# Five blocks of x loaded by four transfers of unequal row counts

## The chip, the cores and the metric

The kernel runs on one core of one Trainium2 chip. The metric is the device time in microseconds; the median of three runs of the kernel before is 1354.09 us (1353.96 to 1354.46). A core has the compute engines PE (matmul), DVE (VectorE), ACT (ScalarE) and GpSimd (POOL), the queue engine SP (SyncE), and 16 DMA engines, which move all data between HBM and the on-chip memory. Transfers are issued on queues: SP's queue appears in the profile as q1, ACT's as q10.

## The reference

For a batch of 4096 rows with 32 fields of 64 numbers, each pair of fields (i, j), i < j, has its own 64 x 64 matrix. Field i is multiplied by the matrix of the pair and the result, elementwise, by field j.

```python
def _L0_rec_ref(inputs, W):          # inputs (4096, 32, 64), W (496, 64, 64), float32
    F = inputs.shape[1]
    idx_i, idx_j = np.triu_indices(F, k=1)      # 496 pairs
    vi = inputs[:, idx_i, :]
    vj = inputs[:, idx_j, :]
    vidots = jnp.einsum('bpd,pde->bpe', vi, W)
    return vidots * vj                # (4096, 496, 64)
```

The input is 33.55 MB of x and 8.13 MB of W; the output is 520.09 MB.

## The kernel before

The batch is cut into 16 blocks of 256 rows. A block stands in the on-chip memory as 128 partitions, each with two batch rows (`NB = 2`); one partition of a block is a contiguous run of 16,384 bytes in HBM. There are two buffers for x. Block 0 and block 1 are loaded by SP's queue at the start, the others, 2 to 15, in the loop by ACT's queue, each in a single transfer of 128 rows.

```python
    xpool = ctx.enter_context(tc.tile_pool(name="xpool", bufs=2))
    tpool = ctx.enter_context(tc.tile_pool(name="tpool", bufs=4))
    opool = ctx.enter_context(tc.tile_pool(name="opool", bufs=3))
    # [cut]
    def new_x(blk: int):
        xs[blk] = xpool.tile([P, 1 + NB * F, D], F32, tag="xs", name=f"xs_{blk}")
        nc.gpsimd.memset(xs[blk][:, 0, :], 0.0)

    def load_x(blk: int, eng, k0: int = 0, k1: int = NB):
        src = rows_of(x, blk).rearrange("(p k) f d -> p (k f) d", k=NB)
        eng.dma_start(out=xs[blk][:, 1 + k0 * F : 1 + k1 * F, :], in_=src[:, k0 * F : k1 * F, :])
    # [cut]
    loads = {place[blk * NB, LATE]: blk + 1 for blk in range(2, NBLK - 1)}   # blocks 3 to 15
    loads[place[LEAD, LATE]] = 2
    # [cut: blocks 0 and 1 and the weights are loaded by SP's queue]
```

A block has two tiles of 128 batch rows (`t`). For each tile the fields are transposed on PE, and for each run of pairs PE multiplies by the weights; DVE, or ACT and GpSimd together, multiply the result by field j and write it to a buffer `ot`. There are three such buffers. A tile's output is cut into five groups of pairs; a group is stored by one transfer on SP's queue, of 128 rows with 23,040, 24,832, 25,344, 26,880 and 26,880 bytes. So a block has ten stores and one load.

```python
    for s, (t, st) in enumerate(sched):
        # [cut]
        if s in loads:
            new_x(loads[s])
            load_x(loads[s], nc.scalar)
        # [cut: transpositions and weights that are due]
        if pa == base:
            ots[t] = opool.tile([P, cap, D], F32, tag="ot", name=f"ot_{t}_{g}")
        # [cut: matmuls into ps]
        if i in aside and c0 == 0 and s not in no_aside:
            tmp = tpool.tile([P, CH, 2, E2], F32, tag="tmp", name=f"tmp_{s}")
            nc.scalar.copy(tmp, src)
            nc.gpsimd.tensor_mul(dst, tmp, xj)
        else:
            nc.vector.tensor_mul(dst, src, xj)
        # [cut]
        if pa + m in ends:
            nc.sync.dma_start(out=..., in_=ot[:, n0 - base : pa + m - base, :])
```

Of the kernel before, what the change touches and what calls it, by code (L numbers as in the profile page):

```python
# [12 lines left out]
def kernel(  # L13
# [16 lines left out]
    nc = tc.nc  # L30

    B, F, D = x.shape
    P = 128
    NB = 2
# [16 lines left out]
    cuts = [*range(0, NP, P), NP]  # L51
# [12 lines left out]
    xs = {}  # L64

    def rows_of(dram: bass.AP, blk: int) -> bass.AP:
        return dram[blk * NB * P : (blk + 1) * NB * P]

    def new_x(blk: int):

        xs[blk] = xpool.tile([P, 1 + NB * F, D], F32, tag="xs", name=f"xs_{blk}")
        nc.gpsimd.memset(xs[blk][:, 0, :], 0.0)  # L72

    def load_x(blk: int, eng, k0: int = 0, k1: int = NB):
        src = rows_of(x, blk).rearrange("(p k) f d -> p (k f) d", k=NB)
        eng.dma_start(out=xs[blk][:, 1 + k0 * F : 1 + k1 * F, :], in_=src[:, k0 * F : k1 * F, :])  # L76


    wflat = w.rearrange("p d e -> p (d e)")
# [4 lines left out]
    def load_w(c: int, eng=nc.sync):  # L84

        a, b = wrows[c]
        pool, tag = ((opool, "ot"), (opool, "ot"), (const, "w3"), (const, "w3"))[c]
        raw[c] = pool.tile([P, D * D], F32, tag=tag, name=f"raw_{c}")
        eng.dma_start(out=raw[c][: b - a, :], in_=wflat[a:b])

    def order_w(c: int, k: int, copy):
        r = wrows[c][1] - wrows[c][0]
        rp = tpool.tile([P, EU, 2, D], F32, tag="tmp", name=f"rp_{c}_{k}")
        src = raw[c][:r, :].rearrange("p (d h e) -> p e h d", h=2, d=D)
        copy(rp[:r], src[:, k * EU : (k + 1) * EU])  # L95
        return rp

    def turn_w(c: int, k: int, rp, copy):
        r = wrows[c][1] - wrows[c][0]
        if c not in wT:  # L100
            wT[c] = const.tile([P, r, E2], F32, tag=f"w{c}", name=f"wT_{c}")
        pt = psum.tile([P, EU, P], F32, tag="ps", name=f"ptw_{c}_{k}")
        for n in range(EU):
            nc.tensor.transpose(  # L104
                pt[:, n, :r], rp[:r, n].rearrange("p h d -> p (h d)"), ident[:r, :r]
            )
        copy(wT[c][:, :, k * EU : (k + 1) * EU], pt[:, :, :r].rearrange("p e r -> p r e"))  # L107

    def turn_x(blk: int, k: int, q: int, copy):

        pt = psum.tile([P, RUN, P], F32, tag="ps", name=f"ptx_{blk}_{k}_{q}")
        for n in range(RUN):
            s = k * F + q * RUN + n
            nc.tensor.transpose(  # L114
                pt[:, n, :], xs[blk][:, s : s + 2, :].rearrange("p f d -> p (f d)"), ident
            )
        xT = xtpool.tile([P, RUN, P], F32, tag="xT", name=f"xT_{blk}_{k}_{q}")
        copy(xT, pt)  # L118
        return xT
# [41 lines left out]
    loads = {place[blk * NB, LATE]: blk + 1 for blk in range(2, NBLK - 1)}  # L161
    loads[place[LEAD, LATE]] = 2

    new_x(0)
    load_x(0, nc.sync, 0, 1)
    load_w(0)
    load_w(1)
    load_x(0, nc.sync, 1, NB)
    load_w(2)
    new_x(1)  # L170
    load_x(1, nc.sync)

    v, p, a = nc.vector.tensor_copy, nc.gpsimd.tensor_copy, nc.scalar.copy
# [9 lines left out]
    for s, (t, st) in enumerate(sched):  # L183
        blk, kt = divmod(t, NB)
        g, i, c0, m = steps[st]
        if s in loads:
            new_x(loads[s])
            load_x(loads[s], nc.scalar)
        for what, *args in due.get(s, ()):
            if what == "x":  # L190
                xT[tuple(args)] = turn_x(*args, a)
            elif what == "turn":
                turn_w(*args, rps.pop(tuple(args)), a)
            else:
                c, k = args
                rps[c, k] = order_w(c, k, (v, v, p, v)[c] if k % 2 == 0 else (v, v, p, a)[c])
                if (c, k) == (2, NU - 1):
                    load_w(3, nc.scalar)

        base, end = groups[g]  # L200
        pa = p0[i] + c0
        if pa == base:
            ots[t] = opool.tile([P, cap, D], F32, tag="ot", name=f"ot_{t}_{g}")
        ot = ots[t]
        ps = psum.tile([P, 2, CH, E2], F32, tag="ps", name=f"ps_{s}")
        for c, (lo, hi) in enumerate(wrows):
            lo, hi = max(pa, lo), min(pa + m, hi)
            if lo < hi:
                for h in range(2):
                    n = i + 1 - h  # L210
                    nc.tensor.matmul(  # L211
                        ps[:, h, lo - pa : hi - pa, :],
                        xT[blk, kt, n // RUN][h * D : (h + 1) * D, n % RUN, :],
                        wT[c][h * D : (h + 1) * D, lo - wrows[c][0] : hi - wrows[c][0], :],
                        start=True,
                        stop=True,
                    )
        o = pa - base
        j = 1 + kt * F + i + 1 + c0
        dst = ot[:, o : o + m, :].rearrange("p m (h e) -> p m h e", h=2)  # L220
        src = ps[:, :, :m, :].rearrange("p h m e -> p m h e")
        xj = xs[blk][:, j : j + m, :].rearrange("p m (h e) -> p m h e", h=2)
# [7 lines that stand above are left out]
        ends = (p0[2], end) if s < NS and (t, g) == (0, 0) else (end,)  # L230
        if pa + m in ends:
            n0 = p0[2] if len(ends) > 1 and pa + m == end else base
            nc.sync.dma_start(  # L233
                out=rows_of(out, blk).rearrange("(p k) n d -> p k n d", k=NB)[:, kt, n0 : pa + m, :],
                in_=ot[:, n0 - base : pa + m - base, :],
            )
# [27 lines left out]
```

## Time and profile before

| what | value |
|---|---|
| time, median of 3 | 1354.09 us |
| span of the profiled execution | 1353.3 us |
| mean granted TensorE clock | 0.948 |
| moved from and to HBM | 562.92 MB in DMA packets, mean 416 GB/s |
| x loads by ACT's queue | 14 of 2048 KB, 16.6 us each from issue to landing (median) |
| stores by SP's queue | 161, 16.4 us from issue to landing (median) |
| issue of an x load on ACT | 351 ns (median) |

How to read it: the profile counts, for each engine, the time in which it had an instruction at work. "Share of 16 engines" in the DMA rows is the time that packets took, divided by 16 times the span. A row of the waits names the engine and line that stood idle, what released it, the total time, the number of times and the longest. The trace also has a record for each DMA packet (queue, start, duration, bytes). A row of a transfer is one packet; each DMA engine that took part in a transfer leaves one more record, of 4 bytes, when its share is done. The records do not name the DMA engine.

### The profile page before, as it was taken

How to read it: one execution, taken by the hardware profiler on the slowest of the kernel's cores; microseconds unless marked ns; L12 is line 12 of the kernel's file. 1: busy time of each engine (PE TensorE's matmuls, PEld its weight loads, DVE VectorE, ACT ScalarE, POOL GpSimd, SP SyncE). 2: the span in 40 equal slices, each digit the busy share in tenths (PEclk: the TensorE clock that was granted, in tenths of full speed). 3: DMA queues.
4: the chain of work that ended last, by engine and by line, in shares of the span. 5: the costliest groups of instructions: out<-in, count | busy, mean ns of one | idle time of the engine just before them, and what ended most of it. 6: DMA issues, size and time to landing. Idle time of an engine off the chain costs nothing.

```text
span 1353.3 us, 17856 instructions
## 1 busy us (share of the span) xinstructions
PE 1180.3 (87%) x7424; PEld 690.9 (51%) x7424; DVE 956.9 (71%) x1262; ACT 374.1 (28%) x367; POOL 530.2 (39%) x246
## 2 busy tenths in 40 slices
PE   6989889889799897988879989888987989988994
PEld 4556545545455454555445545454554545545552
DVE  5778768767677676776757777676775767767774
ACT  3432222222232232222222222222222222223221
POOL 1813424444243443433444334433434434344431
PEclk9989999989999898999989999899998999989997
DMA  9999999999999999999999999999999999999997
GB/s 386 370 426 408 424 427 431 428 432 431 418 414 419 433 412 418 422 413 426 428 407 422 417 425 410 423 421 407 425 410 426 419 422 427 401 432 428 415 417 319
DMA packets 26273, 562.92 MB, mean 416 GB/s; under 512 B 2912, under 2 KB 2912, under 8 KB 3040
## 3 DMA queue, kind: packets, MB, share of 16 engines
q1 hardware_dynamic: 24048, 530.59, 92.4%
q10 hardware_dynamic: 2144, 31.20, 5.5%
q8 instruction: 58, 0.95, 0.3%
q14 instruction: 23, 0.19, 0.0%
HBM read 41.68 MB, written 520.09 MB: 415 GB/s over the span
## 4 chain that ended last, share of the span: by engine, by line
DMA 50%; PE 25%; DVE 17%; POOL 3%; issue 2%; ACT 0%; DVEq 0%; SPq 0%; POOLq 0%; ACTq 0%
DMA out_dram<-ot 50%; PE ps L211 20%; DVE ot L228 17%; PE ptx L114 4%; POOL ot L226 3%; PE ptw L104 1%; DMA raw<-in_L_rec_W_dram 1%; ACT tmp L225 0%; DVE rp L95 0%; POOL rp L95 0%; DVEq L228 0%; ACT wT L107 0%; SPq L76 0%; POOLq L226 0%; SPq L233 0%
## 5 line engine op out<-in xcount | busy, mean ns | idle before, releaser
L228 DVE TENSOR_TENSOR ot<-ps,xs 128x1024 f32<-128x1024 f32 (+15 forms) x1252 | 945.6, 808 | 364.7 <-DMA out_dram<-ot 185.9
L211 PE MATMUL ps<-wT,xT 64*128 64x512 f32 (+13 forms) x6272 | 1034.9, 473 | 132.8 <-DVE ot L228 121.3
L211 PEld LDWEIGHTS ps<-wT,xT 64*128 64x128 f32 x6272 | 563.7, 197 | 569.9 <-DVE ot L228 306.8
L226 POOL TENSOR_TENSOR ot<-tmp,xs 128x1024 f32<-128x1024 f32 x220 | 519.6, 2362 | 647.4 <-ACT tmp L225 457.1
L225 ACT COPY tmp<-ps 128x1024 f32<-128x1024 f32 x220 | 222.7, 1012 | 500.1 <-PE ps L211 459.6
L118 ACT COPY xT<-ptx 128x1024 f32<-128x1024 f32 x128 | 129.6, 1012 | 428.2 <-PE ptx L114 428.2
L114 PE MATMUL ptx<-ident,xs 128*128 128x128 f32 x1024 | 141.2, 281 | 18.5 <-DVE ot L228 9.9
L114 PEld LDWEIGHTS ptx<-ident,xs 128*128 128x128 f32 x1024 | 111.0, 142 | 64.3 <-issue 44.1
L72 POOL MEMSET xs<- 128x64 f32 x16 | 2.4, 152 | 148.6 <-DVE ot L228 148.6
L104 PE MATMUL ptw<-ident,rp 128*128 128x128 f32 (+1 forms) x128 | 19.2, 305 | 3.9 <-DVE rp L95 3.9
L104 PEld LDWEIGHTS ptw<-ident,rp 128*128 128x128 f32 (+1 forms) x128 | 16.2, 160 | 10.3 <-DVE rp L95 5.0
L107 ACT COPY wT<-ptw 128x1024 f32<-128x1024 f32 (+1 forms) x15 | 14.8, 984 | 21.4 <-PE ptw L104 21.4
L95 DVE COPY rp<-raw 128x1024 f32<-128x1024 f32 (+1 forms) x9 | 10.7, 1219 | 11.1 <-DMA raw<-in_L_rec_W_dram 11.1
L95 POOL COPY rp<-raw 128x1024 f32<-128x1024 f32 x4 | 8.0, 1994 | 0.1
L95 ACT COPY rp<-raw 112x1024 f32<-112x1024 f32 (+1 forms) x3 | 5.9, 1959 | 5.1 <-POOL ot L226 3.3
L107 DVE COPY wT<-ptw 128x1024 f32<-128x1024 f32 x1 | 1.2, 1224 | 3.3 <-PE ptw L104 3.3
L118 ACT ACT_TABLE_LOAD x1 | 1.3, 1283 | 0.7 <-PEq L251 0.7
masks.py:197 POOL MEMSET ident<- 128x128 f32 x1 | 0.2, 206 | 0.3 <-POOLq L251 0.3
masks.py:199 POOL TENSOR_SCALAR_AFFINE_SELECT ident<-ident 128x128 f32<-128x128 f32 x1 | 0.3, 295 | 0.0
L251 POOL MEMSET const-float32-0.0<- 128x1 f32 x1 | 0.1, 99 | 0.2 <-issue 0.2
L251 POOL MEMSET const-bfloat16-1.0<- 128x1 bf16 x1 | 0.1, 102 | 0.0
L251 POOL MEMSET const-uint8-127<- 128x1 uint8 x1 | 0.1, 102 | 0.0
(1 smaller groups left out, 0.1 us busy)
## 6 DMA issues: line engine op xcount, KB each, us to landing
out_dram<-ot SPq DMA_DIRECT2D x64, 3360.0 KB, 16.2
out_dram<-ot SPq DMA_DIRECT2D x32, 3168.0 KB, 15.4
out_dram<-ot SPq DMA_DIRECT2D x32, 3104.0 KB, 17.0
out_dram<-ot SPq DMA_DIRECT2D x31, 2880.0 KB, 16.4
xs<-in_r_inputs_dram ACTq DMA_DIRECT2D x14, 2048.0 KB, 16.6
raw<-in_L_rec_W_dram SPq DMA_DIRECT2D x3, 2048.0 KB, 14.3
xs<-in_r_inputs_dram SPq DMA_DIRECT2D x2, 1024.0 KB, 10.9
xs<-in_r_inputs_dram SPq DMA_DIRECT2D x1, 2048.0 KB, 24.6
```

The source lines that it names most:

```text
L72: nc.gpsimd.memset(xs[blk][:, 0, :], 0.0)
L95: copy(rp[:r], src[:, k * EU : (k + 1) * EU])
L104: nc.tensor.transpose(pt[:, n, :r], rp[:r, n].rearrange("p h d -> p (h d)"), ident[:r, :r])
L107: copy(wT[c][:, :, k * EU : (k + 1) * EU], pt[:, :, :r].rearrange("p e r -> p r e"))
L114: nc.tensor.transpose(pt[:, n, :], xs[blk][:, s : s + 2, :].rearrange("p f d -> p (f d)"), ident)
L118: copy(xT, pt)
L211: nc.tensor.matmul(ps[:, h, lo - pa : hi - pa, :], xT[blk, kt, n // RUN][h * D : (h + 1) * D, n % RUN, :], wT[c][h * D : (h + 1) * D, lo - ...
L225: nc.scalar.copy(tmp, src)
L226: nc.gpsimd.tensor_mul(dst, tmp, xj)
L228: nc.vector.tensor_mul(dst, src, xj)
L251: nc = _bacc.Bacc("TRN2", target_bir_lowering=False, num_devices=1)
```

## The change

The x load takes a list of row cuts. For block numbers that leave remainder 1 when divided by 3, the load in the loop is made by four transfers of 96, 25, 5 and 2 rows instead of one of 128; all four are issued on ACT's queue, one after the other. Its words say what it is for: "five of sixteen x blocks loaded by four transfers of ACT's queue with 96, 25, 5 and 2 rows, so that the first five DMA engines load more rows". What is computed stays the same, and so do all stores.

```diff
-    def load_x(blk: int, eng, k0: int = 0, k1: int = NB):
+    def load_x(blk: int, eng, k0: int = 0, k1: int = NB, cuts=(0, P)):
         src = rows_of(x, blk).rearrange("(p k) f d -> p (k f) d", k=NB)
-        eng.dma_start(out=xs[blk][:, 1 + k0 * F : 1 + k1 * F, :], in_=src[:, k0 * F : k1 * F, :])
+        for a, b in zip(cuts[:-1], cuts[1:]):
+            eng.dma_start(
+                out=xs[blk][a:b, 1 + k0 * F : 1 + k1 * F, :], in_=src[a:b, k0 * F : k1 * F, :]
+            )
+
+
+
+    UNEVEN = (0, 96, 121, 126, P)
 
@@
             new_x(loads[s])
-            load_x(loads[s], nc.scalar)
+            load_x(loads[s], nc.scalar, cuts=UNEVEN if loads[s] % 3 == 1 else (0, P))
```

## The prediction

> **What bounds the kernel now.** I read the page from the top: busy shares, then the DMA rows, the DMA queues, the chain that ended last, then the waits and, last, the single DMA records of the trace.
>
> ```profile
> span 1353.3 us, 17856 instructions
> PE 1180.3 (87%) x7424; PEld 690.9 (51%) x7424; DVE 956.9 (71%) x1262; ACT 374.1 (28%) x367; POOL 530.2 (39%) x246
> DMA  9999999999999999999999999999999999999997
> ...
> q1 hardware_dynamic: 24048, 530.59, 92.4%
> q10 hardware_dynamic: 2144, 31.20, 5.5%
> q8 instruction: 58, 0.95, 0.3%
> ...
> DMA 50%; PE 25%; DVE 17%; POOL 3%; issue 2%; ACT 0%; DVEq 0%; SPq 0%; POOLq 0%; ACTq 0%
> ```
>
> No compute engine is at its limit: the busiest, PE, has 87%. The 16 DMA engines have at least nine tenths in every slice but the last, and SP's queue (q1, the stores) and ACT's queue (q10, the x loads and one weight load) fill 97.9% of their time. So the bytes bound the kernel. The waits say through which buffers:
>
> ```profile
> DVE ot L228 <- DMA out_dram<-ot: 185.9, 84, 5.8
> ...
> POOL ot L226 <- DMA out_dram<-ot: 153.1, 59, 5.5
> ```
>
> DVE and GpSimd wait for a store to land, because the result goes through three buffers and a buffer is free only when its store has landed on all its DMA engines. The steady stage, over four blocks of x (compare columns five to eight, DMA share and GB/s):
>
> ```profile
> core 0: us, PE busy (x) PEld busy (x) DVE busy (x) ACT busy (x) POOL busy (x), PEclk, DMA share, GB/s
> 286.00:369.00 83.00, 72.51 (x456) 42.12 (x456) 58.91 (x78) 22.27 (x22) 33.07 (x15) 0.96 1.00 427
> 369.00:451.60 82.60, 74.07 (x456) 43.76 (x456) 58.68 (x78) 22.27 (x22) 33.18 (x15) 0.92 0.99 419
> 451.60:533.70 82.10, 72.75 (x456) 42.03 (x456) 59.02 (x78) 22.27 (x22) 33.21 (x15) 0.95 0.98 416
> 533.70:617.00 83.30, 72.34 (x456) 42.16 (x456) 58.64 (x78) 22.27 (x22) 33.23 (x15) 0.95 1.00 423
> ```
>
> One block takes about 82.7 us, of which PE is busy 73 us. The rest is a wait for stores.
>
> The page gives no time for each DMA engine, so I took the records apart. Each store leaves 16 small records of 4 bytes, one when each engine ends its share. From store 46 on (about 369 us) the median distance from the first of the 16 to the eighth is 0.1 us, to the fifteenth 1.7 us, to the sixteenth 6.3 us (5.2 to 9.5). So a single engine is far behind all others, always. Following the records that join end to end before such a last ending gives its rows:
>
> ```
> row of 26,880 bytes: 1,020 to 1,067 ns   (most other engines: 996)
> row of 23,040 bytes:   855 to   893 ns   (most other engines: 855)
> row of 16,384 bytes:   611 to   636 ns   (most other engines: 611)
> ```
>
> It is never idle in this stage: its next row starts 6 ns after the end of a store. The others are: they end a store 6 us earlier and wait until the slow one has set a buffer free. A block on an undisturbed engine is two times eight rows of 855, 921, 940, 996 and 996 ns and eight rows of 611 ns, less 3.5 ns for each row (they overlap by so much): 80.0 us. The measured 82.7 us is what the slow engine needs, 30 ns more for each of its 88 rows. So the time is the slow engine's sum of rows, and the other fifteen have up to 2.7 us of slack in a block.
>
> **What the Trainium skill says.** "DMA: Bandwidth & Descriptors", section "Why a DMA increments its semaphore by 16 and not by 1": a transfer from ACT's queue runs on the largest k up to 16 that divides its rows, and on the lowest-numbered k engines. No transfer of the kernel before shows a k below 16. Same page, "Queues, rings and completion order": an engine takes turns between its queues. The trace agrees: while an x load runs, rows of 996 ns and of 611 ns alternate on an engine. Same page, "Latency and other measured facts": engines 7 and 15 are usually slower than the rest in traces. The trace shows one slow engine; its records carry no number.
>
> **The change part by part.** By that rule 96 rows give 6 to each of 16 engines, 25 rows give 5 to each of engines 0 to 4, 5 rows one more to each of these, 2 rows one more to engines 0 and 1:
>
> ```
> engine      0, 1    2, 3, 4    5 to 15
> before       8         8          8
> after       13        12          6
> ```
>
> Bytes and the computation stay the same. The condition is a block number with remainder 1 by 3, and the load in the loop is called for blocks 2 to 15: that is 4, 7, 10 and 13. Block 1, the fifth of the title, is loaded ahead of the loop by SP's queue in one transfer. So four blocks change, not five. The built program agrees: ACT has 12 instructions more, three for each of four blocks.
>
> 1. Removed on engines 5 to 15: 4 blocks x 2 rows x 0.62 us (the slow engine's 611 to 636 ns) = 5.0 us each.
> 2. Added on engines 0 and 1: 4 x 5 x 0.611 = 12.2 us; on 2 to 4: 4 x 4 x 0.611 = 9.8 us. If none is the slow one this lies in their slack: 12 stages of about 82.7 us with up to 2.7 us each, some 32 us.
> 3. ACT: 12 more issues of about 351 ns (the median of its x loads) = 4.2 us in all; ACT is busy 28%, so nothing on the path.
> 4. New waits: the built program gives each small transfer a DMA semaphore, and makes it wait for that semaphore's earlier user, a store some eight transfers back. With three buffers that store has landed by then. The first transposition of such a block waits for four transfers in place of one, which land within about 25 us, when the block is needed only some 70 us after. Nothing.
> 5. A passing collision: after an uneven load engines 0 and 1 are 5 x 0.61 = 3.05 us later than before, the slow one 1.24 us earlier. It was 5.6 us behind the mass in the first store after a load, so it is 4.4 us behind, while 0 and 1 are at 3 to 4 us. Mostly the slow one still ends last. If an instruction fetch falls on 0 or 1 just then (a fetch held up its engine by about 1.8 us in the records at 432 us), it may cost a few tenths. I take 0.4 us in all.
>
> Sum, with the slow engine among 5 to 15: 1354.1 - 5.0 + 0.4 = 1349.5 us, 0.34% less.
>
> **The rivals.** (a) The slow engine is one of 0 to 4. Then its sum grows by 9.8 or 12.2 us, all on the path: 1364 to 1366 us. For it: when the stores start from rest, all 16 engines start within about 151 ns, in two groups, 7 within 32 ns and 9 from 53 ns on; in the steady stage the first group shows at most six, so the slow engine starts among the first seven. If they start in the order of their numbers, it is one of 0 to 6. Against it: the skill's page points at 7 and 15, the order may have nothing to do with numbers, and the split at exactly five engines makes sense only to someone who had seen the slow one above. I give it 17%. (b) The others are the bound anyway, through the collisions of step 5 or because engines 0 and 1 stay late: then the gain shrinks to 0 to 3 us, 1351 to 1354. Against it: 2.7 us of slack a block, and two even blocks after each uneven one. (c) PE or DVE take over as soon as stores are quicker: PE needs 73 of 82.7 us, and the gain is 1.2 us in each of four blocks; no room for this rival.
>
> **Range and chances.** The main case gives 1349 to 1350, a full gain without collisions 1349, a slow engine that gains more than its rows because its lag is shorter perhaps 1348; rival (b) up to 1354; rival (a), beyond, is the tail. I predict 1349.5 us, with 1347.5 to 1358 as the range for 8 in 10. A change of over 2% is 27 us either way, twice what the largest term can do: faster by over 2% 0.005, within 2% 0.985, slower 0.01.
>
> **What would show it.** In the changed kernel: ACT's x loads as ten of 128 rows and four each of 96, 25, 5 and 2; in the records of an uneven load, five engines with 12 or 13 rows of 16,384 bytes and eleven with 6; the sixteenth ending of a store still single and late, and the blocks with an uneven load about 1.2 us shorter, the others unchanged. If those blocks are 2.4 to 3.1 us longer, the slow engine is one of the first five. If they are no shorter and two engines end last together, it was the collision. A small transfer that lands 16 engines' worth of rows on more than five would make the row counts, and with them all terms, wrong.

## The result and the profile after

The changed kernel takes 1366.88 us (median of 4 runs, 1366.47 to 1367.77); the kernel before, run beside it, takes 1354.28 us (1353.96 to 1354.55). The ratio is 1.0094, with a 95% interval of 1.0077 to 1.0112. That is 12.6 us longer, where 4.6 us shorter was predicted: within 2%, but outside the range.

The page of the changed kernel, with the rows that were shown of the kernel before: span, busy shares, DMA slices, the queues (packets, MB, share of 16 engines) and the chain that ended last.

```profile
span 1364.9 us, 17876 instructions
PE 1185.5 (87%) x7424; PEld 692.4 (51%) x7424; DVE 957.4 (70%) x1262; ACT 374.0 (27%) x367; POOL 529.6 (39%) x246
...
DMA  9999999999999999999999999999999999999997
...
q1 hardware_dynamic: 24048, 530.59, 91.7%
q10 hardware_dynamic: 2192, 31.20, 5.5%
q8 instruction: 58, 0.95, 0.3%
...
DMA 49%; PE 27%; DVE 17%; POOL 4%; issue 2%; ACT 0%; DVEq 0%; SPq 0%; POOLq 0%; ACTq 0%
```

Nothing here looks like a new bound. Busy times of the compute engines and bytes are as before. Only q10 has 48 packets more: each engine that takes part in a transfer leaves an end record, and four loads in four parts leave 4 x (16 + 5 + 5 + 2) = 112 of them in place of 4 x 16 = 64. So 25 rows ran on five engines, 5 rows on five and 2 rows on two, as the rule that the prediction cited from the Trainium skill says ("DMA: Bandwidth & Descriptors", "Why a DMA increments its semaphore by 16 and not by 1"). The records count the engines but do not number them; the numbers below are those of the rule, by which a transfer takes the lowest. The waits are the old ones too (engine and line, what released it: us in all, times, longest; the change moves the lines by seven):

```profile
DVE ot L235 <- DMA out_dram<-ot: 177.4, 75, 5.8
POOL ot L233 <- DMA out_dram<-ot: 154.7, 59, 5.5
```

The loads are where the difference is. First the issues by size (issues, KB of each), then all issues of that line (times, then shortest, median and longest in ns, and first and last start in us):

```profile
xs<-in_r_inputs_dram ACTq DMA_DIRECT2D x10, 2048.0 KB
...
xs<-in_r_inputs_dram ACTq DMA_DIRECT2D x4, 1536.0 KB
...
xs<-in_r_inputs_dram ACTq DMA_DIRECT2D x4, 400.0 KB
...
xs<-in_r_inputs_dram ACTq DMA_DIRECT2D x4, 80.0 KB
xs<-in_r_inputs_dram ACTq DMA_DIRECT2D x4, 32.0 KB
```

```profile
L77 ACTq DMA_DIRECT2D xs<-in_r_inputs_dram x26: 285/364/1697, 135.7 to 1187.8; - x26
```

Four loads are split, not five, and the 26 issues are 12 more than before, at a median of 364 ns. Now four stages of one block each, the first and the fourth with a split load (columns as in the prediction):

```profile
core 0: us, PE busy (x) PEld busy (x) DVE busy (x) ACT busy (x) POOL busy (x), PEclk, DMA share, GB/s
274.40:360.10 85.70, 76.82 (x464) 44.31 (x464) 59.04 (x78) 23.04 (x23) 33.15 (x15) 0.90 0.98 415
360.10:442.90 82.80, 72.83 (x456) 41.95 (x456) 58.76 (x78) 22.34 (x23) 33.15 (x15) 0.96 0.99 419
442.90:525.50 82.60, 71.69 (x448) 40.85 (x448) 58.84 (x78) 21.43 (x22) 33.18 (x15) 0.96 0.99 418
525.50:610.80 85.30, 73.28 (x464) 43.08 (x464) 58.86 (x78) 22.97 (x23) 33.19 (x15) 0.96 0.97 408
```

The split blocks take 85.7 and 85.3 us, the others 82.8 and 82.6, and the DMA share of the split ones falls to 0.98 and 0.97, GB/s to 415 and 408: fifteen engines wait longer for one. The last endings of every tenth store, from the records, show it over the whole span:

```
us from one block's last ending to the next
before  83.29 82.68 82.07 83.25 82.67 82.69 83.23 82.67 82.69 82.65 82.68 80.25 77.67
after   85.73 82.71 82.64 85.35 82.68 82.65 85.68 82.68 83.05 86.55 82.04 80.85 77.66
        split             split             split             split
```

The four split blocks are longer by 2.44, 2.10, 2.45 and 3.90 us, 10.9 in all. The prediction had named the sign: longer by 2.4 to 3.1 us if the slow engine is one of the first five. Two of the four lie in that range, one below and one above. The slow engine's own records, end to end in the split block from 525.5 us on, say which rows it had. Before and between them lie rows of stores, not listed.

```
row of the 96-row transfer      613, 611, ... six in all, end record at 528.730
rows of the 25-row transfer     611, 618, 611, 611, 611,  end record at 537.828
row of the 5-row transfer       685,                      end record at 539.517
the 2-row transfer              no row and no end record
```

Six, five and one are 12 rows, and no share in the last transfer. By the rule this is engine 2, 3 or 4: the slow engine is among those that were given more rows.

### The profile page after: what moved, and what is told of

Read it like the earlier page. It is cut to its first block, busy times and chain, and to the rows that moved or that the text cites. A ratio compares the mean times of both kernels' runs of the same rounds, so it can differ in the third digit from the quotient of the medians.

```text
span 1364.9 us, 17876 instructions
## 1 busy us (share of the span) xinstructions
PE 1185.5 (87%) x7424; PEld 692.4 (51%) x7424; DVE 957.4 (70%) x1262; ACT 374.0 (27%) x367; POOL 529.6 (39%) x246
## 4 chain that ended last, share of the span: by engine, by line
DMA 49%; PE 27%; DVE 17%; POOL 4%; issue 2%; ACT 0%; DVEq 0%; SPq 0%; POOLq 0%; ACTq 0%
DMA out_dram<-ot 48%; PE ps L218 22%; DVE ot L235 16%; PE ptx L121 4%; POOL ot L233 3%; PE ptw L111 1%; DMA raw<-in_L_rec_W_dram 1%; DVE rp L102 0%; ACT tmp L232 0%; POOL rp L102 0%; DVEq L235 0%; ACT wT L114 0%; POOLq L233 0%; SPq L77 0%; SPq L240 0%
## 5 line engine op out<-in xcount | busy, mean ns | idle before, releaser
L121 PE MATMUL ptx<-ident,xs 128*128 128x128 f32 x1024 | 145.0, 286 | 34.6 <-DVE ot L235 26.1
L121 PEld LDWEIGHTS ptx<-ident,xs 128*128 128x128 f32 x1024 | 114.1, 145 | 81.3 <-issue 41.4
```

What stands on the lines that cost most here:

```text
L121: nc.tensor.transpose(pt[:, n, :], xs[blk][:, s : s + 2, :].rearrange("p f d -> p (f d)"), ident)
```

## Experiments

The theories at the start: **A**, the slow engine has one of the numbers 2 to 4, and its four more rows of 0.62 us per split block are the loss (9.9 us of 12.6); **B**, the collision, in which engines 0 and 1 with 13 rows end last; **C**, the splitting itself costs, whatever the rows.

**Splitting with equal rows.** The same four blocks, four transfers of 32 rows: 8 rows for every engine, as before.

```diff
-    UNEVEN = (0, 96, 121, 126, P)
+    UNEVEN = (0, 32, 64, 96, P)
```

> The same four blocks, again by four transfers, but of 32 rows each, so that every DMA engine loads 8 rows as before. Theory A (the slow engine is number 0 or 1, and the time is its sum of rows): no change, 1353 to 1356 us. Theory B (two engines with 13 rows hold up the stores, whichever engine is slow): no change either. Theory C (four transfers, their issues, semaphores and waits cost the time): about +12.6 us as in the change, 1367 us.

Measured: 1359.94 us (1359.83 to 1360.27) against 1354.66, ratio 1.004 (1.0023 to 1.0056). That is 5.3 us, 1.3 per split block for three further transfers, so neither 0 nor 12.6: each further transfer costs about 0.44 us though no row is added. In the slow engine's records, x rows around the start of a further transfer took 739, 1053 and 880 ns where others take 611, and one row of a store 1244 where 996 is usual.

**One row more on the first engine only**, in all 14 loads of the loop: 112, 14, 1 and 1 rows give engine 0 ten rows, engines 1 to 13 eight, 14 and 15 seven.

```diff
-    UNEVEN = (0, 96, 121, 126, P)
+    UNEVEN = (0, 112, 126, 127, P)
@@
-            load_x(loads[s], nc.scalar, cuts=UNEVEN if loads[s] % 3 == 1 else (0, P))
+            load_x(loads[s], nc.scalar, cuts=UNEVEN)
```

> All 14 blocks loaded in the loop by four transfers of 112, 14, 1 and 1 rows: engine 0 loads 10 rows, engines 1 to 13 load 8, engines 14 and 15 load 7. Theory A with engine 0 the slow one: 14 x 2 rows x 0.63 us = +17.6 us, 1372 us. Theory A with engine 1 the slow one: no change, 1354 us. Theory B: no change, for two rows more (1.2 us) lie within the 2.7 us of slack that an engine of usual speed has in a block. Theory C: 14/4 of the change's loss, +44 us, 1398 us.

Measured: 1367.89 us (1367.03 to 1368.93), ratio 1.0099 (1.0084 to 1.0114): 13.2 us or 0.94 per block, which by time alone is nearest to what was expected if the slow one is engine 0. The records say otherwise: the slow engine had eight x rows, not ten, so it isn't engine 0. Its one row of the second transfer took 1038 ns in place of 611 and the store row after it 1258 in place of 996. These two, 0.69 us, are most of the 0.94. So a transfer with one row on an engine costs that engine more than the row, and a time that fits an expectation can come from another term.

**The change in all 14 loads** of the loop.

```diff
-            load_x(loads[s], nc.scalar, cuts=UNEVEN if loads[s] % 3 == 1 else (0, P))
+            load_x(loads[s], nc.scalar, cuts=UNEVEN)
```

> The change's four transfers in all 14 blocks loaded in the loop. Theory A: five rows more on the slow engine in each block, 14 x 5 x 0.63 = +44 us, 1398 us. Theory B: two even blocks no longer follow, so two engines of usual speed need 80.0 + 3.05 = 83.1 us for a block in place of 82.7, +0.4 us a block: about +6 us, 1360 us. Theory C: +44 us, so that C and A are told apart by the other runs.

Measured: 1393.2 us (1392.53 to 1394.28), ratio 1.0286 (1.0271 to 1.0301): 38.5 us, or 2.75 per load. Nearly all steady blocks take 85.1 to 85.6 us. B falls: were it a passing collision, it would not grow with every load. Four rows of 0.62 us make 2.5 of the 2.75.

**Stores only.** 160 stores from three constant buffers; no loads and no computation. The question is whether one engine is slow by itself.

```diff
+    bufs = [const.tile([P, cap, D], F32, tag=f"st{n}", name=f"st{n}") for n in range(3)]
     for s, (t, st) in enumerate(sched):
-        # [cut: all loads, transpositions, matmuls and multiplications are left out]
+        if pa + m == end:
+            nc.sync.dma_start(out=..., in_=bufs[n % 3][:, : end - base, :])
```

> Leaves out all loads and all computation: 160 stores of the kernel's shapes from three buffers that are filled once, in the kernel's order. On an engine of usual speed these are 16 blocks x 75.1 us = 1202 us. If one engine is slower by itself (30 ns a row), the time is about 1202 + 1280 x 0.030 = 1240 us plus some 10 us of start, and the sixteenth ending of a store falls further and further behind the others, by more than 20 us at the end. If the slowness comes from the computation (its instructions, semaphores or on-chip traffic), the 16 endings stay within 3 us and the time is about 1212 us.

Measured: 1220.67 us, and the 16 endings of the last store lie within 0.3 us. No engine is slow by itself. What is late in the full kernel comes from something beside the stores, which the probes below look for.

**Which number.** The cuts make transfers of 96, 25, 4 and 3 rows in the four blocks, so that engines 0 to 2 have 13 rows, engine 3 has 12 and engine 4 has 11.

```diff
-    UNEVEN = (0, 96, 121, 126, P)
+    UNEVEN = (0, 96, 121, 125, P)
```

> The change with its last two transfers of 4 and 3 rows in place of 5 and 2: engines 0 to 2 load 13 rows, engine 3 loads 12, engine 4 loads 11, the others 6. In the changed kernel the records of the slow engine show 12 rows and no part in the transfer of 2 rows, so it should be 2, 3 or 4. If it is 2, its records show 13 rows, and the time is 4 x 0.62 = 2.5 us above the changed kernel's, 1369 us; if 3, 12 rows and the same time, 1367 us; if 4, 11 rows and 2.5 us less, 1364 us. The rival, that engines 0 and 1 with their 13 rows set the time, expects no difference, 1367 us, and the last ending of each store on an engine with 13 rows.

Measured: 1362.72 us (1362.43 to 1362.93) against 1354.49, ratio 1.0063 (1.0046 to 1.0079): 8.2 us. The slow engine's records have the end of the 25-row transfer at 537.18 us, and after it only rows of stores: 11 rows, and no share in the transfers of 4 and 3. So it is the one of the five in the 25-row transfer that takes part in no later one. By the rule it is engine 4, for which 1364 had been expected. Its three further rows make 4 x 3 x 0.62 = 7.4 us; 0.8 us are left for the one further transfer that it takes part in, 0.2 each.

**What makes engine 4 late.** The stores again, each time beside one kind of instruction on constants: all 6,272 weight matmuls; 1,472 multiplications on DVE; 736 copies on ACT with 368 multiplications on GpSimd.

```diff
+        nc.tensor.matmul(ps[:, h, lo - pa : hi - pa, :], xTc[...], wTc[...], start=True, stop=True)   # first
+        nc.vector.tensor_mul(oc[...], pc[...], xc[...])                                               # second
+        if s % 2 == 0: nc.scalar.copy(tc1, pc...)                                                     # third
+        if s % 4 == 0: nc.gpsimd.tensor_mul(oc..., t2..., xc...)                                      # third
```

> The stores alone, as before, beside all matmuls of the kernel that multiply by the weights (on constant data, their results unread); no loads, no DVE, ACT or GpSimd work. The slow engine's rows in the kernel before were the longer the more matmuls ran beside them. Theory P (PE's instructions slow one engine): one engine falls behind, some 30 to 40 ns a row while PE runs, and the time goes from 1220.7 us to 1245 to 1260 us. Rival theory (the work of DVE, ACT or GpSimd, or the loads, slow it): 1221 us and all 16 endings within 0.6 us.

> The stores alone beside one DVE multiplication of the kernel's size for each step, PSUM and on-chip memory as its sources, results unread. Theory P: 1221 us and the 16 endings within 0.6 us. Rival (DVE slows one engine): 1245 us or more and one late ending.

> The stores alone beside ACT copies from PSUM and GpSimd multiplications, somewhat more than in the kernel, results unread. Theory P: 1221 us and the 16 endings within 0.6 us. Rival (ACT or GpSimd slows one engine): 1245 us or more and one late ending.

Measured: 1244.28, 1359.93 and 1222.35 us. In the first, three last endings stand alone, 8.0 us (eight rows) apart, and the last comes 20.1 us after the other engines are done. The PE row of that kernel's 40 slices and its DMA row:

```profile
span 1242.5 us, 12760 instructions
PE 879.8 (71%) x6272; PEld 539.7 (43%) x6272; DVE 15.7 (1%) x4; POOL 6.3 (1%) x7
...
PE   3999999999999999999999999999900000000000
...
DMA  7999999999999999999999999999999999999992
```

PE is done after slice 29 and waits for nothing: the stores and the matmuls share no buffer. Yet the last slice has a DMA share of two tenths, one engine working off its lag. In the second and the third probe the last engine ends 2.5 to 2.7 and 1.7 to 1.8 us late. Here both expectations were missed: the endings are not within 0.6 us, and the third run is far from 1245 us. The time of the second says nothing, since DVE ran for 1302.9 us, longer than the stores; its lag does. Divided by the instructions beside the stores (12,544 with the weight loads, 1,476, about 1,112):

```
beside the stores          instructions   lag, us        ns per instruction
matmuls, weight loads            12,544   20.1 to 23.6   1.6 to 1.9
DVE multiplications               1,476    2.5 to  2.7   1.7 to 1.8
ACT copies, GpSimd mult.          1,112    1.7 to  1.8   1.5 to 1.6
```

The lower figure counts from the last endings of the other engines (in the third probe, where a second engine was 0.9 us late, of the other fourteen), the higher from the last ending of the stores alone. PE, DVE, ACT and GpSimd, with tiles of different sizes, cost the late engine about the same for each instruction.

The records of the first probe show that the delay lies in the late engine's rows and stops with the instructions. Followed back from its last ending, end to end, to 549 us, it has 359 rows before PE's last matmul ends at 900 us. Each is longer than the quickest of its size, by 13 ns at least and 36 ns on average. Of the 363 rows after that none is longer by more than 4 ns. One of the 359 is longer by over 100 ns (313 ns), though 20 packets of 16,384 bytes that fetch instructions fall into that stretch. So it is not these packets that hold the engine up: the excess is on every row.

**Number or work.** The same matmuls, each with one pair of columns (32 in place of up to 512).

```diff
-  nc.tensor.matmul(ps[:, h, lo - pa : hi - pa, :], xTc[...], wTc[..., lo - wrows[c][0] : hi - wrows[c][0], :], ...)
+  nc.tensor.matmul(ps[:, h, :1, :], xTc[...], wTc[..., :1, :], ...)
```

> The stores beside the same number of matmuls as in the run of stores and PE, but with 32 columns each in place of up to 512, so that PE's busy time and its on-chip traffic fall several-fold while its instructions stay 12,544. There one engine fell 23.6 us behind (1.9 ns an instruction). Theory N (the number of instructions counts): again some 24 us behind while nothing else changes, 1244 us. Rival theory W (PE's work or its data traffic counts): less than a third of it, 1221 to 1229 us.

```profile
span 1243.5 us, 12760 instructions
PE 669.2 (54%) x6272; PEld 669.1 (54%) x6272; DVE 15.7 (1%) x4; POOL 6.3 (1%) x7
...
PE   3999999999999999999999100000000000000000
...
DMA  7999999999999999999999999999999999999992
```

Measured: 1245.26 us. PE's busy time falls from 879.8 to 669.2 us, by a quarter and not several-fold as expected, and it is done six slices earlier, but the late engine's end stays (its last ending 20.9 us after the others). Columns fall up to sixteen-fold and the lag does not, so the number of PE's instructions counts and not the data that they move. The rows say the same. The last 136 rows of the late engine before PE's end at 690 us are 48.5 ns longer on average, where it was 36; PE's instructions come at 18.7 a us in place of 14.3. Both make 2.6 ns of the engine's time for each instruction, counted from its quickest rows. The table has less, because the rows of the other engines are not all of the quickest either (5 ns over it on average in that stretch).

**In the full kernel: half of the matmuls left out.** One half of each pair's outputs is left out; the multiplication reads the other half twice.

```diff
-                for h in range(2):
+                for h in range(1):
-        src = ps[:, :, :m, :].rearrange("p h m e -> p m h e")
+        src = ps[:, 0, :m, :].unsqueeze(2).to_broadcast([P, m, 2, E2])
```

> The kernel before with half of its weight matmuls left out (the second half of each pair's outputs; the multiplication reads the first half twice), so that the output is not the reference's. Loads, stores, DVE, ACT and GpSimd work are as before; PE issues 6,272 instructions less of 17,856. PE is busy 87% and not the bound, so a lighter PE by itself should change nothing: 1354 us. Theory N (each instruction of any engine holds DMA engine 4 up by 1.9 to 2.1 ns, and its sum of rows is the time): 6,272 x 2 ns = 12 to 13 us less, 1342 us, and the sixteenth ending of the stores less late than 6 us or no longer single.

```profile
PE 2018.7 (95%) x4288; PEld 1138.0 (54%) x4288; DVE 1010.3 (48%) x1262; ACT 374.0 (18%) x367; POOL 526.9 (25%) x246
...
PEclk9755555555555555555555555555555555555555
```

Measured: 2126.88 us, ratio 1.5706. Half of the matmuls, and PE is busy 1.7 times as long: the granted clock fell to 0.52 and PE became the bound. The 16 endings of a store lie within 0.16 us (median), but the queue of stores takes only 59.1% of the engines' time here, so each store starts from rest and no lag can gather. On the question, the run says nothing.

**In the full kernel: more instructions.** Behind each of GpSimd's 220 multiplications stand 6, then 12 copies of one number per partition, 1,320 and 2,640 instructions more. GpSimd is idle 61% of the time.

```diff
             nc.gpsimd.tensor_mul(dst, tmp, xj)
+            for r in range(6):          # 12 in the second
+                nc.gpsimd.tensor_copy(few[:, r : r + 1], tmp[:, 0, 0, 0:1])
```

> The kernel before with six more GpSimd copies of one number for each partition behind each of its 220 multiplications: 1,320 instructions more (and what waits they bring) on an engine that is busy 39% and waits for ACT most of the time. Nothing more is loaded, stored or multiplied. Theory N (each instruction of any engine holds DMA engine 4 up by about 2 ns, and that engine is the bound in this kernel too): 1,320 x 2 = +2.6 us, 1357 us. Rival (the effect belongs to the stripped kernels, or to PE alone): no change, 1354 us.

> The same with twelve such copies, 2,640 instructions more. Theory N: +5.3 us, 1360 us, twice the step of the run with six. Rival: no change, 1354 us, or, if GpSimd itself comes onto the path (some 1 us more behind each multiplication), an extra that begins only here and shows as waits for GpSimd before the stores.

Measured: 1358.78 us (1358.63 to 1360.88) against 1354.72, ratio 1.0035 (1.0022 to 1.0047), and 1366.64 us (1365.64 to 1366.87), ratio 1.0088 (1.0074 to 1.0102). A steady block is 0.28 and 0.57 us longer, in proportion to the number. The group of the twelve copies (instructions, busy us, mean ns, idle before), and a stretch of four blocks with the copies:

```profile
L229 POOL COPY few<-tmp 128x1 f32<-128x1 f32 x2640 | 330.3, 196 | 0.0
```

```profile
core 0: us, PE busy (x) PEld busy (x) DVE busy (x) ACT busy (x) POOL busy (x), PEclk, DMA share, GB/s
451.00:783.00 332.00, 291.37 (x1818) 169.92 (x1816) 234.27 (x312) 89.09 (x88) 210.59 (x733) 0.94 0.99 417
```

The same stretch of the kernel before:

```profile
451.00:783.00 332.00, 290.65 (x1824) 168.81 (x1824) 235.79 (x313) 89.08 (x88) 133.29 (x61) 0.95 0.99 419
```

The copies take 77 us of GpSimd in 332, and it has still 121 us free; PE, DVE and ACT are busy as before, but 417 GB/s in place of 419. The objection is that the copies only delay results. The sign that the expectation named for it, waits for GpSimd before the stores, is there: over the whole span the issues of stores wait 49.0 us for the copies with six and 75.3 us with twelve (20.7 us for GpSimd's multiplications before), and the chain that ended last has 23% of GpSimd with twelve copies. In the steady stage the records speak against it. After each last ending of a store the slow engine's next row starts within 20 ns, in both kernels: it is never idle for a result, so its rows must be longer. In rows that can be followed back from its last endings without a second candidate (253 before, 309 with six, 420 with twelve, without a few that are longer by 100 ns or more) the mean excess over the quickest rows is 35, 38 and 41 ns, each with a standard error of about 1 ns. Six asks for 3.2 ns more on 88 rows and twelve for 6.5, and 2.3 and 5.1 are seen, in direction and roughly in size what the block times ask for. These rows all lie near the end of a store, so it is not shown for all 88. By block time a copy costs 0.57 us / (2,640 / 16) = 3.5 ns. The full run with twelve loses 12 us: 13 blocks from about 285 us on make 7.4, and this stage begins 3.9 us later.

The kernel before shows the dependence too, with nothing added. In the same 253 rows of its slow engine the mean excess is 9 ns where fewer than five PE instructions start during the row, 35 ns where 5 to 14 do, and 44 ns where 15 or more do.

**Can it be turned around?** If engine 4 is the late one, it should load fewer rows. One transfer of 112 rows and four of 4 rows give engines 0 to 3 eleven rows and all others seven. First in seven loads, then in all 14.

```diff
-    UNEVEN = (0, 96, 121, 126, P)
+    UNEVEN = (0, 112, 116, 120, 124, P)
@@
-            load_x(loads[s], nc.scalar, cuts=UNEVEN if loads[s] % 3 == 1 else (0, P))
+            load_x(loads[s], nc.scalar, cuts=UNEVEN if loads[s] % 2 == 0 else (0, P))   # second: cuts=UNEVEN
```

> The runs so far say: the slow engine is number 4, it bounds the time by its sum of rows, and a further transfer costs the engines that take part in it some tenths of a us. Here the loads of every second block (2, 4, ... 14: seven blocks) are made by transfers of 112, 4, 4, 4 and 4 rows: engines 0 to 3 load 11 rows, all others 7, and the slow engine takes part in the first transfer alone. Theory (engine 4): 7 x 0.62 = 4.3 us less than before, 1350 us. If the slow engine were one of 0 to 3: 7 x 3 x 0.62 = +13 us and more for the transfers, 1367 us or above. If four small transfers cost time wherever they run: +5 us or more, 1360 us.

> The same in all 14 blocks loaded in the loop. Engine 4 saves 14 x 0.62 = 8.7 us, which by itself gives 1346 us; but engines 0 to 3 have three rows (1.9 us) and four more transfers (some 0.5 us each) a block, with 2.7 us of slack and no even block to catch up in. Theory: about as long as before, 1350 to 1362 us, with the last endings of the stores now on engines 0 to 3. If the slack is larger than thought, 1346 us.

Measured: 1353.19 us (1352.27 to 1354.2) against 1354.43, ratio 0.9989 (0.9977 to 1.0001), and 1360.24 us (1357.59 to 1363.68), ratio 1.0045 (1.0032 to 1.0058). In seven loads the gain is 1.2 us, not told apart from nothing, where 4.3 was expected; most uneven blocks are only about 0.3 us shorter, where the row less is 0.62. Engines 0 to 3 now end 2.4 to 5.9 us late in the stores after such a load, which agrees with their four more rows in four further transfers. In all 14 loads that outweighs the gain. The version with seven such loads is the quickest of the complete kernels here, and it does not clearly beat the kernel before.

## Why the prediction was wrong

**What held.** The bound: the time is the slow engine's sum of rows, and split blocks are longer by what it had to do while the others stayed at 82.7 us. Four blocks change, not five. The rows per engine: 12 on the slow one, and the counts of end records, are as listed. Step 2's slack: engines 0 and 1 had 13 rows, one more than engine 4, and yet a single one with 12 ended last. Step 3: ACT's 12 issues did not show; no engine waits for them. Rival (c) did not appear, and rival (b) fell with the change in all loads.

**The step that failed is step 1**, with the words "with the slow engine among 5 to 15". Engine 4 is the slow one. In place of 5.0 us less on the path come the 9.8 us that step 2 gave to engines 2 to 4 and laid into slack: 4 blocks x 4 rows x 0.62 us = 9.9 us. The evidence had been there: the slow engine started among the first seven of each burst, and the split at five engines made sense to someone who knew. I set against it the Trainium skill's remark that engines 7 and 15 are usually slower ("DMA: Bandwidth & Descriptors", "Latency and other measured facts"). The same row of the page gives a best guess as the cause and ties it to transfers whose descriptors GpSimd writes; the stores and loads here stand in the profile as hardware_dynamic, so the remark was no argument in this case. The runs show number 4 late, and with stores alone no engine (0.3 us).

**The second is step 4's "Nothing"**, a term that I left out. A further transfer costs an engine that takes part more than its rows: 0.2 us per transfer with unequal counts (96, 25, 4, 3), 0.44 with four equal ones, 0.9 for one with a single row. On engine 4 the change adds two transfers per split block, 8 in all; what 9.9 leaves of 12.6 is 2.7 us, 0.34 for each, in the middle of these. This is a remainder and not a measurement: the four split blocks of the profiled run are longer by 10.9 us, which leaves 1.0 us for the transfers, and the rest is lost elsewhere in the run. The sum is

```
4 blocks x 4 rows x 0.62 us                    9.9 us
8 further transfers on engine 4 x 0.34 us      2.7 us   (the remainder; 0.2 to 0.9 in other runs)
total                                         12.6 us
```

Rival (a) said 1364 to 1366, and 1366.9 came out; but its upper figure was that of engines 0 and 1 with five more rows, and the slow engine has four. It came near through the term that was missing.

**What stays open.** Why the instructions of all engines slow one DMA engine. The packets that fetch instructions are not the direct cause (first probe with matmuls). Untested is the recording itself: every run here has a span and a granted clock, so its instructions were recorded one by one. Whether the engine is held up by the instructions or by their records was not told apart, and without recording the lag, and with it the loss of this change, may be another. In the stores-only probes the late engine's number was not determined. No run could give engine 4 fewer rows without further transfers, so a gain from that alone was not tried.

## What to carry to other kernels

On a kernel bound by transfers find out first which DMA engine ends last, by transfers with unequal shares read in the records, before rows are moved from one engine to another: the same split helps or harms by that number alone. Count a further transfer as a cost on each engine that takes part, here 0.2 to 0.9 us, up to more than a row of 16,384 bytes (0.61 us). And where one engine's rows set the time, instructions that lie beside everything else were not free in these recorded runs.

## What the runs showed of the hardware, unexpectedly

One DMA engine is late in proportion to the number of instructions beside the transfers: 1.5 to 1.9 ns for each in the probes, with instructions of four engines, and 3.5 ns for a GpSimd copy in the full kernel by its block time. With stores alone it is not late (0.3 us). An estimate from the traces: a block of the kernel before has some 1,027 instructions (456 matmuls, 456 weight loads, 78, 22 and 15 of DVE, ACT and GpSimd), and the 2.6 ns of the engine's time for each make 2.7 us, about the whole slack of the fifteen others.

The first row of a further transfer took 1038 ns on a busy engine and the store's row after it 1258, where 611 and 996 are usual.

With matmuls of only one half of the rows the granted clock fell to 0.52 and a matmul took 752 ns on average, against 473 before.
